# Where the softmax of the self-attention is divided by its sums: in the probabilities, head by head, instead of in the output

## The chip, the cores and the metric

The kernel runs on one core of a Trainium2 chip. The metric is the device time of one execution in microseconds. The engines are named as in the profile: PE is TensorE (matmul; PEld are its weight loads), DVE is VectorE, ACT is ScalarE, POOL is GpSimd, SP is SyncE, which issues most transfers.

## The reference

One decoder layer over x, 8 batches of 256 rows of 1024 columns: self-attention, cross-attention, feed-forward, each on a layer norm of x and added to x. Only the self-attention is touched by the change:

```python
y = einsum('bsi,oi->bso', x, sign(w / s)) * (s * scale)      # q, k, v and the output projection
scores = einsum('bhqd,bhkd->bhqk', q, k) / sqrt(32)          # 32 heads of 32, 8 key/value heads
attn = softmax(scores, axis=-1)
out = einsum('bhqk,bhkd->bhqd', attn, v)                     # then the output projection
```

The softmax divides each row of exponentials by its sum. As the division is by row (by query), it may be done to the exponentials before the product with v or to the product after it.

## The kernel before

The self-attention is done in 64 steps, one for each batch b (8) and each group c of four heads (8). A `Self` object stands for one step. The function `step(cur, prev, parts)` issues all work of one step in a fixed order; nothing is reordered afterwards, and each engine takes its instructions in the order in which they are issued. Three groups are in flight at once: `cur` gets its scores and exponentials, `prev` (one step older) gets its transposes and its product with v, and `due` (two steps older) gets its output written.

In order, a step issues the following.

- `cur.scores()` (L554): eight matmuls into four PSUM banks `s`, one for each head.
- `due.early()` (L585, L590): two matmuls with the constant `sel` spread the reciprocal sums `rT` (8 rows) over the 128 output rows, into the second half of the bank `po`; ScalarE copies them to `rb`.
- For each head, VectorE's negated row maximum `nm` (L678), and `turned(prev.p[j])` (L535, L539): four transposes of the exponentials on TensorE into one of three PSUM banks, which are also those of the projections, and a copy `pT` by ScalarE.
- `due.late()` (L600, L355, L356): VectorE multiplies the output in `po` by `rb`; ScalarE rounds the product to `oh` and VectorE takes the remainder `ol`. The output projection runs over both, `oh` and `ol`.
- The parts of the step, taken from a queue by `run_part()`: pieces of projections, layer norms and (in batch 0) weight preparation that fill TensorE while ScalarE makes exponentials. Each part carries an estimate of its length `us`. The eight exponentials of the step (`exp`, L697: two halves of rows for four heads, with the row sums collected into `sm`) are placed between the parts by these estimates: a counter `sc` starts at 1.0, grows by 0.49 for each exponential, and is compared with the sum of the parts' estimates. `run_part` also issues pieces of waiting statistics (`idle`, layer norm moments on VectorE), one for each 1.7 of estimated time. After the first part comes `prev.sums()` (L566, L568): a transpose of the eight columns of `sm` on TensorE and a copy `rT` on VectorE.
- `nc.vector.reciprocal(cur.sm, cur.sm)` (L723), and `prev.weighted(pTs)` (L574): the product with v, into the first half of `po`. The pool `pso` holds one buffer only, so `po` of the next group can be written only once that of the last is no longer read.

The usual batch has two long steps (c = 0 and 4, four or more parts of 2.0), two with layer-norm parts (c = 1 and 2) and four short ones (c = 3, 5, 6, 7, two parts of 2.0). `nan_to_num` (L362 to L368) follows each projection with work on VectorE and Pool. Cross-attention (`Cross`) runs through the same `step`, and divides its output in `late` (L659); the feed-forward follows.

Of the kernel before, what the change touches and what calls it, by code (L numbers as in the profile page):

```python
# [10 lines left out]
F32 = mybir.dt.float32  # L11
F32R = mybir.dt.float32r
U8 = mybir.dt.uint8
AF = mybir.ActivationFunctionType
ALU = mybir.AluOpType
# [3 lines left out]
P = 128  # L19
# [16 lines left out]
def decoder_layer(  # L36
# [24 lines left out]
    nc = tc.nc  # L61
    B, S, E = x.shape
    NT = B * S // P
    TB = S // P
# [15 lines left out]
    const = ctx.enter_context(tc.tile_pool(name="const", bufs=1, side="left"))  # L80
# [7 lines left out]
    pso = ctx.enter_context(tc.tile_pool(name="pso", bufs=1, space=PSUM))  # L88
    xin = ctx.enter_context(tc.tile_pool(name="x_in", bufs=4, side="left"))
    wk_ = ctx.enter_context(tc.tile_pool(name="work", bufs=1, side="left"))  # L90

    ident = const.tile([P, P], F32, name="ident")
# [3 lines left out]
    mhalf = const.tile([P, TB], F32, name="mhalf")  # L96
    nc.gpsimd.memset(mhalf, -0.5)

    sel = const.tile([8, TB, P], F32, name="sel")
    nc.gpsimd.memset(sel, 1.0)  # L100
    for t in range(TB):
        nc.gpsimd.affine_select(
            sel[:, t, :], sel[:, t, :], [[1, P]], ALU.is_ge, 0.0,
            base=4 * t * 32, channel_multiplier=-32,
        )
        nc.gpsimd.affine_select(
            sel[:, t, :], sel[:, t, :], [[-1, P]], ALU.is_ge, 0.0,
            base=31 - 4 * t * 32, channel_multiplier=32,
        )


    x1 = dram.tile([NT, P, E], F32, name="x1")
    x2 = dram.tile([NT, P, E], F32, name="x2")

# [23 lines left out]
    idle, credit = [], [0.0]  # L138
# [46 lines left out]
    def settle():  # L185
        now = list(ripe)
        ripe[:] = later
        later.clear()
        for f in now:
            f()  # L190
# [11 lines left out]

    queue = []

    def run_part():

        settle()
        p = queue.pop(0)
        p.ahead()
        if queue:  # L210
            queue[0].ahead()
        p.main()
        credit[0] += p.us
        while idle and credit[0] > 1.7:
            credit[0] -= 1.7
            idle.pop(0)()
        if not idle:
            credit[0] = 0.0
# [135 lines left out]
    def split(hi, lo, src):  # L354
        nc.scalar.copy(hi, src)  # L355
        nc.vector.tensor_sub(lo, src, hi)  # L356
# [174 lines left out]
    def turned(p):  # L531
        ps = bank([P, TB, S], "ps_pt")
        for k in range(TB):
            for t in range(TB):
                nc.tensor.transpose(  # L535
                    ps[:, k, t * P : (t + 1) * P], p[:, t, k * P : (k + 1) * P], ident
                )
        pT = wk_.tile([P, TB, S], F32, tag="pT", name="pT", bufs=4)
        nc.scalar.copy(pT, ps)  # L539
        return pT  # L540

    class Self:


        def __init__(self, st, c):
            self.st, self.c = st, c

        def scores(self):
            st, c = self.st, self.c
            s = [pss.tile([P, TB, S], F32, tag="pss", name="s") for _ in range(4)]  # L550
            for t in range(TB):
                for j in range(4):
                    p0 = 32 * j
                    nc.tensor.matmul(  # L554
                        s[j][:, t, :],
                        st.qT[p0 : p0 + 32, c, t * P : (t + 1) * P],
                        st.kT[p0 : p0 + 32, c // 4, :],
                        start=True,
                        stop=True,
                    )  # L560
            return s

        def sums(self):

            self.po = pso.tile([P, 2, S], F32, tag="pso", name="po")
            nc.tensor.transpose(self.po[:8, 1, :P], self.sm.rearrange("p t j -> p (t j)"), ident)  # L566
            self.rT = wk_.tile([8, P], F32, tag="rT", name="rT")
            nc.vector.tensor_copy(self.rT, self.po[:8, 1, :P])  # L568

        def weighted(self, pTs):  # L570
            for k in range(TB):
                for j in range(4):
                    g, p0 = 4 * (self.c // 4) + j, 32 * j
                    nc.tensor.matmul(  # L574
                        self.po[p0 : p0 + 32, 0, :],
                        self.st.v[:, k, g * HD : (g + 1) * HD],
                        pTs[j][:, k, :],
                        start=(k == 0),
                        stop=(k == TB - 1),
                    )  # L580

        def early(self):

            for t in range(TB):
                nc.tensor.matmul(  # L585
                    self.po[:, 1, t * P : (t + 1) * P], sel[:, t, :], self.rT,
                    start=True, stop=True,
                )
            self.rb = wk_.tile([P, S], F32, tag="rb", name="rb")
            nc.scalar.copy(self.rb, self.po[:, 1, :])  # L590

        def late(self):
            st, c = self.st, self.c
            if c == 0:
                i = st.b % 2
                st.oh, st.ol = [
                    [wk_.tile([P, 4, S], F32R, tag=f"{n}{i}{h}", name=n) for h in "ab"]
                    for n in ("oh", "ol")
                ]
            nc.vector.tensor_mul(self.rb, self.po[:, 0, :], self.rb)  # L600
            split(st.oh[c // 4][:, c % 4, :], st.ol[c // 4][:, c % 4, :], self.rb)

    class Cross:

# [17 lines left out]
                        )  # L622
            return s

        def sums(self):
            pass

        def weighted(self, pTs):
# [39 lines left out]
    def step(cur, prev, parts, extra=None):  # L668

        s = cur.scores()  # L670
        nm = small.tile([P, 4, TB], F32, tag="nm", name="nm")
        cur.sm = small.tile([P, TB, 4], F32, tag="sm", name="sm")
        due = prev.prev if prev is not None else None
        if due is not None:
            due.early()
        pTs = []
        for j in range(4):
            nc.vector.tensor_reduce(nm[:, j, :], s[j], AX.X, ALU.max, negate=True)  # L678
            if prev is not None:
                pTs.append(turned(prev.p[j]))  # L680
        for p in queue[: min(parts, 2)]:
            p.ahead()
        soon = [p for p in queue[:parts] if p.soon][:2]
        if isinstance(due, Cross):
            for p in soon:
                p.ahead()
        if due is not None:
            due.late()
        for p in soon:
            p.ahead()  # L690
        cur.p, cur.prev = [], prev
        exps = []

        def exp(j, t):
            if t == 0:
                cur.p.append(wk_.tile([P, TB, S], F32, tag="p", name="p", bufs=4))
            nc.scalar.activation(  # L697
                cur.p[j][:, t, :], s[j][:, t, :], AF.Exp,
                bias=nm[:, j, t : t + 1], accum_out=cur.sm[:, t, j : j + 1],
            )  # L700

        exps = [(j, t) for j in range(4) for t in range(TB)]


        pe, sc = 0.0, 1.0
        for k in range(parts):
            pe += queue[0].us
            while exps and sc < pe:
                exp(*exps.pop(0))
                sc += 0.49  # L710
            run_part()
            if k == 0 and prev is not None:
                prev.sums()
            if k == 0 and extra is not None:
                extra()
        for e in exps:
            exp(*e)
        if not parts:
            if prev is not None:
                prev.sums()  # L720
            if extra is not None:
                extra()
        nc.vector.reciprocal(cur.sm, cur.sm)  # L723
        if prev is not None:
            prev.weighted(pTs)
            prev.prev = None
        return cur
# [369 lines left out]
    for b in range(B):  # L1097
        for l in (sts, xts):
            st = State()
# [118 lines left out]
    with tc.manual_schedule(  # L1218
# [8 lines left out]
        st = sts[0]  # L1227
# [9 lines left out]
        for q in range(2 * TB):  # L1237
            t, h = q // 2, q % 2
# [30 lines left out]
        prev = None  # L1269
        for kind, sts_, plan, loads, extra, n in (  # L1270
            (Self, sts, self_plan, self_loads, self_extra, EC),
            (Cross, xts, cross_plan, cross_loads, cross_extra, XH // 4),
        ):
            for b in range(B):
                ps_ = plan(b)
                for p in ps_:
                    queue.extend(p)
                for c in range(n):
                    loads(b, c)
                    prev = step(kind(sts_[b], c), prev, len(ps_[c]), extra(b, c))  # L1280


        pairs = [(fb, f) for fb in fbs for f in range(NF)]
# [76 lines left out]
```

## Time and profile before

| | |
|---|---|
| Median of three runs | 1594.41 us (1591.75 to 1595.04) |
| The profiled execution | 1593.47 us |
| Its span in the trace | 1591.8 us |
| Mean granted TensorE clock | 0.994 |
| Self-attention, from its first scores to the first of the cross-attention | 26.3 to 674.3 us |
| Batch 0 | 101.2 us |
| Batches 1 to 7 | 77.1 to 78.9 us each |
| Mean length of steps c = 0 to 7, batches 1 to 6 | 12.3, 9.2, 9.8, 8.6, 12.6, 8.4, 8.4, 8.6 us |

A step's length is the distance between the first weight loads of the scores (L554) of two steps. In the profile a line of the timeline gives start, length, engine, source line, operation, output and inputs, and in brackets the idle time ahead of it with what ended it. A line of the waits gives who waited for whom, the total in microseconds, how many times and the longest. A line of the windows gives the stretch and its length, then for PE, PEld, DVE, ACT and POOL the busy time with the number of instructions, then the granted clock and the transfers. A matmul of 32-bit floats shows as two records for each instruction, and a transpose as one.

### The profile page before, as it was taken

The numbers are of one execution on the slowest core, as the hardware profiler recorded it, in microseconds if no ns is written. First come the engines' busy times: TensorE is split into PE (matmuls) and PEld (weight loads), VectorE is DVE, ScalarE is ACT, GpSimd is POOL, SyncE is SP. The second block draws the span as 40 slices with busy tenths as digits, with TensorE's granted clock in tenths as the row PEclk, the third lists the DMA queues.
The fourth block names the chain that finished last, engine by engine and source line by source line (L and its number), as shares of the span: only waits on it lengthen the run. The fifth ranks groups of instructions, "written<-read, shape, count | busy, mean of one in ns | idle before, by whom it ended". The sixth has DMA issues, their size and how long they took to land.

```text
span 1591.8 us, 25596 instructions
## 1 busy us (share of the span) xinstructions
PE 1550.8 (97%) x9814; PEld 1058.8 (67%) x9814; DVE 905.9 (57%) x1692; ACT 756.7 (48%) x2346; POOL 358.7 (23%) x449
## 2 busy tenths in 40 slices
PE   6899999999999999999999999999999999999998
PEld 6778888888888888777777777544444444444443
DVE  6867787868686877665676666343233323423322
ACT  4777777777777777655655666411111110111110
POOL 2333433333333343112221112100010002001102
PEclk9999999999999999999999999999999999999999
DMA  8420010101010042111154412120002002000001
GB/s 231 88 54 27 15 67 25 57 28 54 28 54 28 28 127 82 54 55 69 56 206 153 135 55 107 40 86 1 0 27 79 0 1 89 17 0 14 40 0 53
DMA packets 65610, 92.78 MB, mean 58 GB/s; under 512 B 40218, under 2 KB 46160, under 8 KB 65360
## 3 DMA queue, kind: packets, MB, share of 16 engines
q1 hardware_dynamic: 60880, 74.37, 14.9%
q0 software_dynamic: 4608, 16.78, 2.6%
q8 instruction: 77, 1.26, 0.3%
q14 instruction: 45, 0.37, 0.1%
HBM read 65.44 MB, written 25.17 MB: 57 GB/s over the span
## 4 chain that ended last, share of the span: by engine, by line
PE 62%; DVE 2%; ACT 0%; issue 0%; POOLq 0%; POOL 0%; DVEq 0%; ACTq 0%
PE ps_h L1019 19%; PE ps_z L1063 9%; PE ps_pt L535 5%; PE s L616 4%; PE po L634 4%; PE ps_p L993 3%; PE ps_o L1082 3%; PE ps_o L503 2%; PE ps_o L651 2%; PE ps_qk L848 2%; PE ps_q L833 2%; PE ps_q L410 1%; PE ps_k L784 1%; PE s L554 1%; PE ps_t L176 1%; PE po L574 1%
## 5 line engine op out<-in xcount | busy, mean ns | idle before, releaser
L697 ACT ACTIVATE p<-s,nm 128x256 f32<-128x256 f32 x768 | 356.9, 503 | 2.2 <-DVE nm L678 2.2
L539 ACT COPY pT<-ps_pt 128x512 f32<-128x512 f32 x384 | 198.2, 600 | 134.1 <-PE ps_pt L535 131.0
L1031 ACT ACTIVATE sg<-ps_h,b_col 128x512 f32<-128x512 f32 (+1 forms) x88 | 59.6, 677 | 413.5 <-PE ps_h L1019 413.5
L678 DVE TENSOR_REDUCE nm<-s 128x2 f32<-128x512 f32 x384 | 236.2, 676 | 12.6 <-PE s L616 6.7
L1032 DVE SCALAR_TENSOR_TENSOR sg<-ps_h,b_col,sg 128x512 f32<-128x512 f32 (+1 forms) x88 | 65.0, 739 | 274.9 <-ACT sg L1031 274.9
L535 PE MATMUL ps_pt<-ident,p 128*128 128x128 f32 x1536 | 195.6, 280 | 1.0 <-DVE xl L356 0.9
L535 PEld LDWEIGHTS ps_pt<-ident,p 128*128 128x128 f32 x1536 | 165.9, 142 | 26.2 <-issue 7.2
L697 ACT ACTIVATION_READ_ACCUMULATOR p<-s,nm 128x1 f32 x768 | 181.0, 236 | 0.0
L1063 PE MATMUL ps_z<-ac,u_sb 128*128 128x512 f32 x336 | 157.7, 593 | 0.0
L1092 POOL TENSOR_TENSOR x2t<-x2t,y 128x512 f32<-128x512 f32 x32 | 40.5, 1267 | 482.5 <-DVE y L1090 482.5
L410 PE MATMUL ps_q<-xh,qT_w 128*128 128x256 f32 x496 | 124.1, 291 | 0.9 <-ACT qT_w L320 0.9
L410 PE MATMUL ps_q<-xl,qT_w 128*128 128x256 f32 x496 | 119.8, 281 | 0.0
L363 POOL TENSOR_SCALAR tmp<-y 128x512 f32<-128x512 f32 x78 | 59.6, 764 | 263.8 <-DVE y L512 154.8
L1063 PEld LDWEIGHTS ps_z<-ac,u_sb 128*128 128x128 f32 x336 | 61.9, 190 | 68.8 <-issue 68.8
L503 PE MATMUL ps_o<-oT_w,oh 128*128 128x512 f32 x256 | 106.9, 417 | 0.0
L503 PE MATMUL ps_o<-oT_w,ol 128*128 128x512 f32 x256 | 101.0, 394 | 0.0
L666 POOL TENSOR_TENSOR x1t<-x1t,y 128x256 f32<-128x256 f32 x64 | 47.5, 762 | 222.9 <-DVE y L659 222.9
L410 PEld LDWEIGHTS ps_q<-xh,qT_w 128*128 128x128 f32 x496 | 93.3, 188 | 3.1 <-ACT qT_w L320 1.1
L410 PEld LDWEIGHTS ps_q<-xl,qT_w 128*128 128x128 f32 x496 | 93.5, 189 | 0.0
L554 PE MATMUL s<-kT,qT 32*128 32x256 f32 x1024 | 88.7, 413 | 2.0 <-ACT p L697 1.0
L1019 PE MATMUL ps_h<-late,w_ffn 128*128 128x512 f32 (+1 forms) x184 | 88.7, 577 | 0.0
L1019 PE MATMUL ps_h<-pT,w_ffn 128*128 128x512 f32 (+1 forms) x184 | 88.7, 577 | 0.0
(165 smaller groups left out, 2706.6 us busy)
## 6 DMA issues: line engine op xcount, KB each, us to landing
xs<-in_x_dram SPq DMA_DIRECT2D x32, 512.0 KB, 3.5
x<-xs POOLq DMA_DIRECT2D x16, 512.0 KB, 3.0
x1t<-x SPq DMA_DIRECT2D x16, 512.0 KB, 5.7
c<-in_ctx_dram SPq DMA_DIRECT2D x16, 512.0 KB, 4.0
x<-x1t POOLq DMA_DIRECT2D x16, 512.0 KB, 3.8
x2t<-x SPq DMA_DIRECT2D x16, 512.0 KB, 5.8
out_dram<-x2t SPq DMA_DIRECT2D x16, 512.0 KB, 2.6
w<-in_L_attn_q_weight_dram SPq DMA_DIRECT2D x32, 128.0 KB, 6.0
```

Source lines behind the costliest of these rows:

```text
L410: nc.tensor.matmul(ps[:, i, :], w(i, e), x_[:, e, :], start=(e == 0 and x_ is st.xh), stop=(e == EC - 1 and x_ is st.xl),)
L503: nc.tensor.matmul(ps, o_[c // 4][:, c % 4, t * P : (t + 1) * P], oT_w[:, c, h * 512 : (h + 1) * 512], start=(c == 0 and o_ is st.oh), sto ...
L535: nc.tensor.transpose(ps[:, k, t * P : (t + 1) * P], p[:, t, k * P : (k + 1) * P], ident)
L539: nc.scalar.copy(pT, ps)
L554: nc.tensor.matmul(s[j][:, t, :], st.qT[p0 : p0 + 32, c, t * P : (t + 1) * P], st.kT[p0 : p0 + 32, c // 4, :], start=True, stop=True,)
L616: nc.tensor.matmul(s[2 * i + j][:, t, :], st.cqk[p0 : p0 + XD, 2 * c + i, t * P : (t + 1) * P], st.ckv[p0 : p0 + XD, :], start=True, stop= ...
L634: nc.tensor.matmul(self.po[XD * j : XD * (j + 1), i, :], self.st.ckvT[:, k, :], pTs[2 * i + j][:, k, :], start=(k == 0), stop=(k == TB - 1),)
L678: nc.vector.tensor_reduce(nm[:, j, :], s[j], AX.X, ALU.max, negate=True)
L697: nc.scalar.activation(cur.p[j][:, t, :], s[j][:, t, :], AF.Exp, bias=nm[:, j, t : t + 1], accum_out=cur.sm[:, t, j : j + 1],)
L1019: nc.tensor.matmul(ps[h * n : h * n + n], v1_of(r, i, f, n), fb.pT[:, r, h * w_ : (h + 1) * w_], start=(r == 0), stop=(r == RC - 1),)
L1032: nc.vector.scalar_tensor_tensor(sg[:m], hs[0][:m], bg, sg[:m], ALU.add, ALU.mult)
L1063: nc.tensor.matmul(fb.zs[r], fw.u2[f // 4][:n, f % 4, r * P : (r + 1) * P], ac[:n], start=(k == 0), stop=(k == NF - 1 and COPIES < 2),)
```

## The change

The exponentials are divided in place, ahead of their transposes, and the transposed sums with all that belongs to them (`sel`, `sums`, `rT`, `rb`) are gone. In each step the reciprocal of the sums is taken for two heads at a time (`over_sums`), and each head is then multiplied by its column of `sm`, on one of three engines by the letter in `by`: P on Pool with one instruction, D on VectorE with two, A on ScalarE with two. The A heads come after all the step's exponentials and parts (`over_sums_end`). The others are issued inside `run_part`, from the second part on, as soon as the exponentials of the pair have been issued, and otherwise after the parts. The output is no longer multiplied: `early` copies it from PSUM to `oh`, and `late` subtracts that from PSUM to give `ol`. The counter `sc` starts at 0.5 in the self-attention, and the statistics are issued for each 1.4 of estimated time, also outside it.

```diff
-    sel = const.tile([8, TB, P], F32, name="sel")
-    nc.gpsimd.memset(sel, 1.0)
...
-    def run_part():
+    def run_part(then=None):
         settle()
+        if then is not None:
+            then()
...
-        while idle and credit[0] > 1.7:
-            credit[0] -= 1.7
+        while idle and credit[0] > 1.4:
+            credit[0] -= 1.4
...
+            self.by = (
+                "AAPP" if st.b == 0 else "DPAA" if c in (1, 2) else "DDAA" if c % 4 == 0 else "DDDA"
+            )
...
-        def sums(self):
-            self.po = pso.tile([P, 2, S], F32, tag="pso", name="po")
-            nc.tensor.transpose(self.po[:8, 1, :P], self.sm.rearrange("p t j -> p (t j)"), ident)
-            self.rT = wk_.tile([8, P], F32, tag="rT", name="rT")
-            nc.vector.tensor_copy(self.rT, self.po[:8, 1, :P])
+        def over_sums(self, pair):
+            heads = range(2 * pair, 2 * pair + 2)
+            r = self.sm[:, :, heads[0] : heads[-1] + 1]
+            nc.vector.reciprocal(r, r)
+            for j in heads:
+                if self.by[j] == "P":
+                    nc.gpsimd.tensor_mul(
+                        self.p[j], self.p[j],
+                        self.sm[:, :, j].unsqueeze(2).to_broadcast([P, TB, S]),
+                    )
+                elif self.by[j] == "D":
+                    for t in range(TB):
+                        p = self.p[j][:, t, :]
+                        nc.vector.tensor_scalar_mul(p, p, self.sm[:, t, j : j + 1])
+
+        def over_sums_end(self):
+            for j in range(4):
+                if self.by[j] == "A":
+                    for t in range(TB):
+                        p = self.p[j][:, t, :]
+                        nc.scalar.activation(p, p, AF.Copy, scale=self.sm[:, t, j : j + 1])
         def weighted(self, pTs):
+            self.po = pso.tile([P, S], F32, tag="pso", name="po")
...
         def early(self):
-            for t in range(TB):
-                nc.tensor.matmul(
-                    self.po[:, 1, t * P : (t + 1) * P], sel[:, t, :], self.rT,
-                    start=True, stop=True,
-                )
-            self.rb = wk_.tile([P, S], F32, tag="rb", name="rb")
-            nc.scalar.copy(self.rb, self.po[:, 1, :])
...
+            nc.scalar.copy(st.oh[c // 4][:, c % 4, :], self.po)
         def late(self):
...
-            nc.vector.tensor_mul(self.rb, self.po[:, 0, :], self.rb)
-            split(st.oh[c // 4][:, c % 4, :], st.ol[c // 4][:, c % 4, :], self.rb)
+            nc.vector.tensor_sub(
+                st.ol[c // 4][:, c % 4, :], self.po, st.oh[c // 4][:, c % 4, :]
+            )
...
-        pe, sc = 0.0, 1.0
+        divided = isinstance(cur, Self)
+        pe, sc = 0.0, 0.5 if divided else 1.0
+        pairs = [0, 1]
         for k in range(parts):
...
-            run_part()
-            if k == 0 and prev is not None:
-                prev.sums()
+            def then():
+                while k and divided and pairs and len(exps) <= 4 - 4 * pairs[0]:
+                    cur.over_sums(pairs.pop(0))
+            run_part(then)
...
         for e in exps:
             exp(*e)
...
-        nc.vector.reciprocal(cur.sm, cur.sm)
+        for i in pairs:
+            cur.over_sums(i)
+        cur.over_sums_end()
```

For the cross-attention `over_sums` takes the one reciprocal where it was before, and `over_sums_end` does nothing.

More of the change, by code (lines that the diff above doesn't have):

```diff
@@ L97, in decoder_layer @@
     nc.gpsimd.memset(mhalf, -0.5)
-    sel = const.tile([8, TB, P], F32, name="sel")
-    nc.gpsimd.memset(sel, 1.0)
-    for t in range(TB):
-        nc.gpsimd.affine_select(
-            sel[:, t, :], sel[:, t, :], [[1, P]], ALU.is_ge, 0.0,
-            base=4 * t * 32, channel_multiplier=-32,
-        )
[L106 to L109, printed above, removed]
     x1 = dram.tile([NT, P, E], F32, name="x1")
@@ L574, in weighted @@
                     nc.tensor.matmul(
-                        self.po[p0 : p0 + 32, 0, :],
+                        self.po[p0 : p0 + 32, :],
                         self.st.v[:, k, g * HD : (g + 1) * HD],
@@ L582, in early @@
         def early(self):
-            for t in range(TB):
-                nc.tensor.matmul(
-                    self.po[:, 1, t * P : (t + 1) * P], sel[:, t, :], self.rT,
-                    start=True, stop=True,
-                )
-            self.rb = wk_.tile([P, S], F32, tag="rb", name="rb")
-            nc.scalar.copy(self.rb, self.po[:, 1, :])
-        def late(self):
             st, c = self.st, self.c
@@ L599, in late @@
                 ]
-            nc.vector.tensor_mul(self.rb, self.po[:, 0, :], self.rb)
-            split(st.oh[c // 4][:, c % 4, :], st.ol[c // 4][:, c % 4, :], self.rb)
+            nc.scalar.copy(st.oh[c // 4][:, c % 4, :], self.po)
+        def late(self):
+            st, c = self.st, self.c
+            nc.vector.tensor_sub(
+                st.ol[c // 4][:, c % 4, :], self.po, st.oh[c // 4][:, c % 4, :]
+            )
     class Cross:
@@ L623, in scores, with over_sums, over_sums_end @@
             return s
-        def sums(self):
+        def over_sums(self, pair):
+            if pair:
+                nc.vector.reciprocal(self.sm, self.sm)
+        def over_sums_end(self):
             pass
@@ L717, in step @@
             exp(*e)
[L718 to L722, printed above, removed]
-        nc.vector.reciprocal(cur.sm, cur.sm)
+        for i in pairs:
+            cur.over_sums(i)
+        cur.over_sums_end()
+        if not parts and extra is not None:
+            extra()
         if prev is not None:
```

## The prediction

> **What bounds the kernel now.** I read the page's busy table first, then a table of busy time for one batch of the self-attention, then the timeline of one of its steps engine by engine, then the waits of TensorE.
>
> ```profile
> PE 1550.8 (97%) x9814; PEld 1058.8 (67%) x9814; DVE 905.9 (57%) x1692; ACT 756.7 (48%) x2346; POOL 358.7 (23%) x449
> 282.70:360.90 78.20, 77.54 (x701) 64.34 (x697) 59.68 (x121) 57.38 (x192) 29.45 (x30) 1.00 0.12 42
> ```
>
> The second line is batch 3 (eight steps, from its first scores to the next batch's): TensorE (first pair) is busy 77.5 of 78.2 us, VectorE (third) 59.7, ScalarE (fourth) 57.4, Pool 29.5. Batches 2 to 6 read alike within 0.2 us. TensorE sets the pace, but the two others have only 20 us a batch to spare, 2.5 us a step. One step, batch 3's seventh, on TensorE:
>
> ```profile
> 342.90 1.07 PE L574 MATMUL po<-pT,v 128*32 128x256 f32 x16
> 343.90 1.20 PE L554 MATMUL s<-kT,qT 32*128 32x256 f32 x16
> 344.87 0.60 PE L585 MATMUL po<-rT,sel 8*128 8x128 f32 x4
> 345.40 1.99 PE L535 MATMUL ps_pt<-ident,p 128*128 128x128 f32 x16
> 347.22 0.38 PE L410 MATMUL ps_q<-xh,qT_w 128*128 128x256 f32 x1
> ...
> 349.10 0.28 PE L410 MATMUL ps_q<-xl,qT_w 128*128 128x256 f32 x1
> 349.21 0.27 PE L566 MATMUL po<-ident,sm 128*8 128x128 f32 x1
> 349.24 0.36 PE L410 MATMUL ps_q<-xh,qT_w 128*128 128x256 f32 x1
> 349.44 0.27 PE L410 MATMUL ps_q<-xl,qT_w 128*128 128x256 f32 x1
> ...
> 352.31 1.07 PE L554 MATMUL s<-kT,qT 32*128 32x256 f32 x10
> ```
>
> Columns are start, length, operation. There is no gap: weighted sums, scores, the broadcast of the sums (L585), the transposes of four heads, 32 projection matmuls, 8.41 us from scores to scores. Matmuls overlap, so a cost is the distance from one start to the next, not a length. ScalarE in the same step:
>
> ```profile
> 343.68 0.24 ACT L697 ACTIVATION_READ_ACCUMULATOR p<-s,nm 128x1 f32 x1
> 345.55 0.37 ACT L590 COPY rb<-po 128x256 f32<-128x256 f32 x1 [1.64 <-issue]
> 346.10 2.06 ACT L539 COPY pT<-ps_pt 128x512 f32<-128x512 f32 x4 [0.17 <-PE ps_pt L535]
> 348.01 0.44 ACT L355 CAST oh<-rb 128x256 fp32r<-128x256 f32 x1
> ```
>
> After its last exponential ScalarE stands 1.64 us, until TensorE has done L585. That hole recurs in most steps (idle before L590: 99.0 us in 48 steps by L590's own record). VectorE has its hole too: its subtraction L356 waits for oh in all 64 steps, 37.9 us together. And what TensorE waits for:
>
> ```profile
> PEld s L554 <- ACT p L697: 14.3, 38, 0.6
> PEld po L566 <- DVE rb L600: 5.4, 7, 1.4
> PEld po L574 <- DVE rT L568: 1.9, 1, 1.9
> ```
>
> **The change part by part.** The sum is made against the profiled execution, 1593.47 us (span 1591.76 and 1.7 around it); the median of the runs is 0.94 above that.
>
> *Removed from TensorE.* L585 (two instructions a step, four passes): 344.87 to 345.40, 0.53 us, the same in other steps. L566: the pair 349.10 to 349.24 holds one normal spacing of 0.11, and the next spacing is 0.20 for 0.12, so it costs 0.03 + 0.08 = 0.11 us. Together 0.64 x 64 steps = 41.0 us. Part of the L585 distance may be the turn from short to full rows, which stays: four plain spacings of 0.113 give 0.45, then 36 us. I take 38.
>
> *Waits removed.* L566 waited for L600, because both use the one bank of po, 5.4 us; the weighted sums once waited for rT, 1.9 us. Both vanish: 7. In short steps (four microseconds of projections) the eighth exponential now stands ahead of the two y copies of the projection on ScalarE instead of behind them, since the count starts at 0.5 for 1.0; the scores no longer wait for it: of the 14.3 us of weight-load waits about 5 are real (the scores' start in 352.31 against the end of the weighted sums), the rest is hidden by the pipeline. Gains so far 38 + 7 + 5 = 50.
>
> *Added to ScalarE.* "A" heads, two activations each: 2 x 2 in batch 0's steps, two heads in steps 0, 1, 2, 4 of the others and one in steps 3, 5, 6, 7, 24 instructions a batch. Nearest row: y<-ps_q (L419, a copy scaled by a column, 128x256), 504 ns long, in pairs 0.36 apart. So 0.36 x 24 = 8.6 us a batch; removed is rb (8 x 0.37 = 3.0). ScalarE goes from 57.4 to 63 of about 73. In the step above they fit the hole: weighted sums 1.0, scores 1.0, the first head's transposes 0.45 and the hand-over 0.17 make 2.6 us from the end of the parts to the first pT copy; ahead of it ScalarE has two y (0.17 + 0.80), one A head 0.72, oh 0.37: 2.1. With two A heads and no y after the exponentials 2.1 likewise; with two and y, 2.8, in the first step of a batch only, where it costs 0.2. oh is copied from PSUM as soon as the weighted sums are there, ahead of the transposes' copies, where formerly it lay after them: nothing behind it waits longer.
>
> *Added to VectorE.* "D" heads: two multiplications each, 36 a batch. The nearest row is kT<-kT (L447, 128x256, 293 ns); xn (L168, two columns as operands) stands 0.455 apart where z<-y (L362, constants, same size) stands 0.343, so a column costs about 0.11; 0.21 + 0.11 = 0.32 us each, 11.5 us. One more reciprocal a step, 8 x 0.11. Removed: rT 8 x 0.2, rb 8 x 0.35. Net 8 us, 60 to 68 of 73. But the subtraction no longer stands waiting for oh (37.9/64 = 0.6 a step, 4.7 a batch) nor rT for L566 (16.3 us in all), so the time to get through VectorE's queue grows by 1 to 2 us a batch only. New are two waits in the queue: each reciprocal waits for the exponentials of its pair, and behind it stand the output multiplication of the projection (it frees a PSUM bank), z, fin and the next step's maxima. In a short step the second reciprocal can run about when the parts end, and delays those by the one D head, 0.6 us; the maxima are then done 1 us later, still before the last pT copy, which the exponentials follow anyway. The steps with layer normalization (1 and 2) are VectorE's fullest, 8.7 of 9.2; they receive one D head only, and the count of 1.4 for 1.7 moves two statistics instructions (0.65 each) out of step 1 into the two before it.
>
> *Added to Pool.* "P" heads, a product of 128x512: nearest row the sums L364, 1.32 us; two a step in batch 0 and one in steps 1 and 2. Heads 2 and 3 are transposed 3.2 us after the parts end at the earliest, and their exponentials end before the last part: 2.6 + 0.3 is covered. Pool is busy 29 of 78. The five instructions for sel at the start go: they lie beside the loads, nothing. SP's queue is unchanged.
>
> *A rule that speaks against it.* Six times v<-y took 0.83 us on VectorE where z<-y of the same shape takes 0.426:
>
> ```profile
> 178.89 0.83 DVE L362 TENSOR_SCALAR v<-y 128x512 f32<-128x512 f32 x1
> 178.16 1.27 POOL L517 TENSOR_TENSOR xs<-xs,z 128x512 f32<-128x512 f32 x1 [0.85 <-DVE z L368]
> ```
>
> Pool's addition had started and ended at 179.43; v ended 0.29 later. The Trainium skill, "SBUF — State Buffer", "Who interferes with whom", says why: both share a port pair, and a VectorE instruction in a two-port mode waits for the whole of a Pool instruction that came first. The D products are of this kind. By the plain rows the sum has 0 for this; by the rule each group of D products can be held up by the rest of a Pool instruction: Pool is busy 3.3 of 8.4 us in a short step, so 0.4 x 0.6 = 0.25 us a group, some 3 us of VectorE a batch. It has 5 to spare. I take 2 us on the path for all batches.
>
> *New waits in all.* Batch 0, where ScalarE ends each step with weight copies and four A products for the heads that are transposed first: 0.5 a step, 4. Steps 1 and 2 of six batches, 0.3 each, 4. The first step of seven batches 0.2, and the port 2: 3.5. Total 11.5; bounds 0 and 40.
>
> Sum: 1593.5 - 50 + 11.5 = 1555; beside the median 1556, rounded towards less gain, **1557 us**.
>
> **The rivals.**
> *Half of it eaten.* ScalarE becomes the bound in short steps: 8 exponentials 3.6, four pT copies 1.9, y 0.8, A 0.72, oh 0.37 = 7.4 us for a TensorE step of 7.75. If an A product costs 0.5 (its length, not its spacing) and the reciprocal's answer comes 0.3 late, that is 8.0, and only 0.4 of 8.41 is gained; the fuller steps 1 and 2 gain nothing. 28 short steps x 0.4 + 28 others x 0.2 = 17: 1577. For it: ScalarE's queue is in order. Against: the 1.64 us hole.
> *Slower, by the port pair.* If each group of D products meets a fresh Pool instruction (1.3 us, two groups a short step), VectorE's short step is 6.0 + 1.5 + 2.6 = 10.1 us, and TensorE waits for the maxima and the divided heads: +1.7 in 28 short steps, 48, while the other 36 save 0.6 each, 22, and 10 of other waits vanish: about 1610. It decides once the mean block exceeds some 1.6 us a short step. Against: z<-y shows 426 ns in all 32, and in the step above Pool runs from 343.86 to 346.03 and from 350.54 to 351.83, of which only the second touches the time of the products.
> *The change does not do what it says:* the transposes start late because the division now lies between exponentials and transposes, yet TensorE had nothing to do there anyway, so no change. It would need over 2.6 us of division after the last exponential in nearly all steps; 1594.
>
> **How the numbers follow.** Main case 0.70 (1545 to 1568); still better, all waits gone, 0.04 (1540); half eaten 0.14 (1568 to 1588); no change 0.03; slower 0.09. The range 1542 to 1583 holds the main case and most of the second. Faster by over 0.2% (3.2 us, about what a measurement of this kernel can tell from no change) 0.88, same 0.03, slower 0.09.
>
> **What would show it.** Right: a short step of 7.7 to 7.9 us on TensorE with scores followed by transposes at once; a batch of 73 to 74.5; A products 0.36 apart in the former hole; VectorE busy near 68 a batch and no wait before its subtraction. Wrong: TensorE's weight loads of the transposes waiting for p from VectorE, ScalarE or Pool by more than 12 us in total; D products of 0.7 us or more beside Pool; steps 1 and 2 longer than 9.2. Cross-attention and feed-forward (from 674 us on) should be as long as before.

## The result and the profile after: 21 us gained of the 37 forecast

| | before | after |
|---|---|---|
| Median of four runs | 1593.08 us | 1571.75 us (1571.54 to 1573.56) |
| Ratio | | 0.9868 (95% interval 0.9851 to 0.9885) |
| Span of the profiled execution | 1591.8 us | 1569.9 us |
| Batch 0 | 101.2 us | 108.3 us |
| Batch 1 | 77.1 us | 73.3 us |
| Batches 2 to 6, each | 78.2 us | 74.5 us |
| Batch 7 | 78.8 us | 74.2 us |
| Cross-attention, first to last scores | 334.7 us | 333.0 us |

The gain is 21.3 us by the medians. It lies inside the range of the prediction (1542 to 1583), but 15 us above its number, 1557, and outside the 1545 to 1568 that the main case gave itself. By size it fell among the values of the rival "half of it eaten"; whether by its mechanism is settled below. Steps are numbered by c from here on: step 6 is the seventh of a batch.

The page after, with the line of busy time, and the row of batch 3 in the table of stretches (stretch, length, then PE, PEld, DVE, ACT and POOL busy, granted clock, transfers):

```profile
PE 1513.1 (96%) x9494; PEld 1015.9 (65%) x9494; DVE 973.0 (62%) x1880; ACT 811.4 (52%) x2482; POOL 390.5 (25%) x474
281.68:356.20 74.52, 72.68 (x660) 59.26 (x656) 68.74 (x150) 63.96 (x207) 31.85 (x32) 1.00 0.12 44
```

TensorE lost 37.7 us of work over the span, of which only 21.9 came off the span: TensorE waits more than before. VectorE stands at 68.7 a batch and ScalarE at 64.0, where the prediction had 68 and 63. Batch 3's step 6 on TensorE, to be laid beside the one shown for before:

```profile
340.43 1.15 PE L547 MATMUL s<-kT,qT 32*128 32x256 f32 x16
341.50 1.99 PE L524 MATMUL ps_pt<-ident,p 128*128 128x128 f32 x16
343.32 0.39 PE L399 MATMUL ps_q<-xh,qT_w 128*128 128x256 f32 x1
...
347.10 0.28 PE L399 MATMUL ps_q<-xl,qT_w 128*128 128x256 f32 x1
347.31 1.07 PE L584 MATMUL po<-pT,v 128*32 128x256 f32 x16
348.31 0.50 PE L547 MATMUL s<-kT,qT 32*128 32x256 f32 x4
```

The transposes follow the scores at once. The step lasts 348.31 - 340.43 = 7.88 us; it lasted 8.41. Here the change does what it says. What the other engines do just then:

```profile
340.11 0.18 DVE L560 RECIPROCAL sm<-sm 128x4 f32<-128x4 f32 x1 [0.40 <-ACT p L708]
340.33 0.91 ACT L577 ACTIVATE p<-p,sm 128x256 f32<-128x256 f32 x2 [0.25 <-DVE sm L560]
340.40 0.62 DVE L570 TENSOR_SCALAR p<-p,sm 128x256 f32<-128x256 f32 x2
341.14 0.35 ACT L601 CAST oh<-po 128x256 fp32r<-128x256 f32 x1
342.19 2.05 ACT L528 COPY pT<-ps_pt 128x512 f32<-128x512 f32 x4 [0.70 <-PE ps_pt L524]
```

The A products and `oh` stand in ScalarE's former hole, and 0.70 us of it is left. The three D heads are divided by 341.02, before their transposes.

TensorE's waits up to the cross-attention's start, by contrast, hold three entries that were nothing, 1.1 and 0.3 us before (total, times, longest):

```profile
PE ps_pt L524 <- ACT pT L528: 6.6, 8, 1.1
PE ps_d L334 <- POOL dg L327: 6.4, 2, 4.0
PE ps_t L163 <- DVE xn L155: 4.4, 6, 0.8
```

They belong to three places: batch 0, the step after a long one (c = 1, 9.23 to 9.66 us in batches 2 to 6), and the step after the layer norms (c = 3, 8.64 to 9.03). A fourth is batch 7. The experiments take them one by one.

### The profile page after: what moved, and what is told of

Same layout as the page of the kernel before. It is cut to its first block, busy times and chain, and to the rows that moved or that the text cites. A ratio compares the mean times of both kernels' runs of the same rounds, so it can differ in the third digit from the quotient of the medians.

```text
span 1569.9 us, 25667 instructions
## 1 busy us (share of the span) xinstructions
PE 1513.1 (96%) x9494; PEld 1015.9 (65%) x9494; DVE 973.0 (62%) x1880; ACT 811.4 (52%) x2482; POOL 390.5 (25%) x474
## 4 chain that ended last, share of the span: by engine, by line
PE 77%; DVE 14%; ACT 6%; DMA 1%; issue 1%; POOL 0%; SPq 0%; POOLq 0%; DVEq 0%; ACTq 0%
PE ps_h L1034 19%; PE ps_z L1078 9%; PE ps_pt L524 8%; PE ps_o L492 5%; PE ps_q L399 5%; PE s L622 4%; PE po L645 4%; PE ps_p L1008 4%; DVE nm L689 4%; PE ps_o L1097 3%; ACT p L708 3%; PE s L547 2%; PE po L584 2%; PE ps_o L662 2%; PE ps_qk L863 2%; DVE p L570 2%
## 5 line engine op out<-in xcount | busy, mean ns | idle before, releaser
L524 PEld LDWEIGHTS ps_pt<-ident,p 128*128 128x128 f32 x1536 | 164.4, 141 | 51.8 <-issue 21.9
L708 ACT ACTIVATION_READ_ACCUMULATOR p<-s,nm 128x1 f32 x768 | 189.8, 247 | 0.0
L1107 POOL TENSOR_TENSOR x2t<-x2t,y 128x512 f32<-128x512 f32 x32 | 40.5, 1267 | 482.5 <-DVE y L1105 482.5
L570 DVE TENSOR_SCALAR p<-p,sm 128x256 f32<-128x256 f32 x252 | 99.0, 448 | 9.6 <-DVE sm L560 1.4
L577 ACT ACTIVATE p<-p,sm 128x256 f32<-128x256 f32 x200 | 87.8, 512 | 17.8 <-DVE sm L560 17.6
```

Source lines behind the costliest of these rows:

```text
L524: nc.tensor.transpose(ps[:, k, t * P : (t + 1) * P], p[:, t, k * P : (k + 1) * P], ident)
L570: nc.vector.tensor_scalar_mul(p, p, self.sm[:, t, j : j + 1])
L577: nc.scalar.activation(p, p, AF.Copy, scale=self.sm[:, t, j : j + 1])
L708: nc.scalar.activation(cur.p[j][:, t, :], s[j][:, t, :], AF.Exp, bias=nm[:, j, t : t + 1], accum_out=cur.sm[:, t, j : j + 1],)
```

## The experiments

### Batch 0: what stands behind Pool's products

Pool's timeline in batch 0's first step, and the matmuls that stand next on TensorE:

```profile
33.75 2.04 POOL L563 TENSOR_TENSOR p<-p,sm 128x512 f32<-128x512 f32 x2 [0.21 <-DVE sm L560]
35.77 1.22 POOL L327 TENSOR_SCALAR dg<-ident,scol 128x128 f32<-128x128 f32 x2
33.65 0.41 PE L466 MATMUL ps_v<-vT_w,xl 128*128 128x256 f32 x1
36.45 1.39 PE L334 MATMUL ps_d<-dg,ones 128*128 128x128 f32 x4 [2.39 <-POOL dg L327]
```

`dg` is a diagonal of weight scales that the look-ahead of a part (`ahead`) lays on Pool. `run_part` issues the division of a pair (`then`) before that look-ahead. So `dg`, which was ready to be made, stands in Pool's queue behind two products that wait for exponentials. In c = 6 the same wait lasts 4.0 us.

A second loss sits on it. The granted clock in the same stretches, after:

```profile
32.00:42.40 10.40, 7.33 (x33) 6.53 (x33) 2.07 (x6) 2.58 (x9) 4.45 (x10) 0.51 0.82 162
117.40:124.40 7.00, 4.77 (x24) 3.94 (x28) 3.35 (x5) 1.06 (x2) 5.83 (x8) 0.51 0.00 0
```

The clock (third number from the end) is half for about 10 and 7 us, and the L466 matmuls stand 0.21 us apart instead of 0.12. Before had 0.85 and 1.00 in these two rows. The experiment moves one call:

```diff
     def run_part(then=None):
         settle()
-        if then is not None:
-            then()
         p = queue.pop(0)
...
             queue[0].ahead()
+        if then is not None:
+            then()
         p.main()
```

> The changed kernel with the in-place division of a pair issued after the look-ahead work of the parts instead of before it, so that in batch 0 the diagonal tiles dg stand ahead of the P products in Pool's queue. Theory (Pool's queue: TensorE waits for dg behind products that wait for exponentials, 6.4 us in two steps, and its clock is then granted at half for 6.8 us more twice): the first and seventh step of batch 0 come from 18.6 and 17.3 to about 14 and 13, batch 0 from 108.3 to 97, the time from 1571.7 to about 1561. Rival (batch 0 loses because the A products for the heads that are transposed first end too late): batch 0 stays at 105 or more, time 1569 or more. Batches 1 to 7 alike in both.

Measured: 1565.69 us (ratio 0.9831, 0.9817 to 0.9846), batch 0 101.7 us (steps 0 and 6: 18.61 and 17.29 became 14.29 and 13.44, before had 13.84 and 13.43), the other batches as after. The same two stretches and the wait that is left, of this kernel:

```profile
32.00:42.40 10.40, 9.59 (x70) 8.57 (x71) 5.40 (x11) 5.52 (x16) 6.41 (x14) 0.84 0.84 173
117.40:124.40 7.00, 6.59 (x62) 5.28 (x54) 4.84 (x9) 6.17 (x20) 4.58 (x9) 1.00 0.01 2
```

```profile
PE ps_d L334 <- POOL dg L327: 1.9, 3, 1.1
```

The order on Pool's queue is the cause of 6.6 of the 7.1 us that batch 0 had lost, 6.1 us of the median, and most of the half clock in these two stretches went with the waits; the rival, A products that end too late, wanted 105 us or more for the batch. It is not all that was expected (97 us): step 7 grew from 8.78 to 10.38, and why was not looked into.

### How much there was to gain, and what the division costs

```diff
-            for j in heads:
+            for j in ():
...
-            for j in range(4):
+            for j in ():
```

> The changed kernel with the products by the reciprocal sums left out on all three engines (the reciprocals are still taken), so the output is not divided: what the removal from TensorE and the removed waits are worth with none of the added work but the reciprocals. If the prediction's gains of 50 us were sized right: 1543 to 1546. If the removal was over-sized (36 for the two groups of matmuls and little for the waits): 1553 to 1557.

Measured: 1553.03 us (0.9752, 0.9733 to 0.9770). Batch 0 is 99.7 us, batches 2 to 6 73.6, batch 7 69.4. So without any product 40 us are gained, not 50; and the division costs 1571.75 - 1553.03 = 18.7 us. By the batches' lengths it is 8.6 in batch 0, about 5 in batches 1 to 6 together, and 4.8 in batch 7.

This kernel also tells which of the late steps the division causes: c = 3 falls from 9.03 to 7.94, but c = 1 is 9.59 without one product. So the products do not make c = 1 late.

### The two counts, without the rest

The first of these puts both new counts into the kernel before, the second only the exponentials' 0.5.

```diff
-        while idle and credit[0] > 1.7:
-            credit[0] -= 1.7
+        while idle and credit[0] > 1.4:
+            credit[0] -= 1.4
...
-        pe, sc = 0.0, 1.0
+        pe, sc = 0.0, 0.5 if isinstance(cur, Self) else 1.0
```

> The kernel before with the two counts of the change alone: exponentials placed from 0.5 instead of 1.0 in the self-attention, statistics for each 1.4 instead of 1.7. The division stays in the output. If the counts bring part of the gain by themselves (scores no longer wait for the last exponential, as the prediction had it): the short steps lose up to 0.2 us and the time is 1588 to 1591. If the statistics' new place costs as in the changed kernel: the second step grows by some 0.5 and the time is 1593 to 1596.

Measured: 1601.16 us (1.0069, 1.0050 to 1.0089). Its waits:

```profile
PEld po L566 <- DVE rb L600: 17.5, 21, 2.4
PE po L566 <- DVE rb L600: 11.2, 6, 2.0
```

The page of before had 5.4 in the first of these rows. The sums' transpose writes the bank that `rb` is read from, so TensorE was tied to VectorE's place in its queue; more work ahead of `rb` on VectorE makes TensorE wait.

> The kernel before with the one count of the exponentials, 0.5 for 1.0 in the self-attention. The prediction put 5 us on the scores that no longer wait for the last exponential. If that was right by itself: 1586 to 1588. If only the fourth and eighth steps of a batch change, as in the run with both counts (0.2 and 0.15): 1589 to 1591. If it costs in other steps: 1593 or more.

Measured: 1596.10 us in 12 runs (1.0020, 1.0009 to 1.0031), no gain and if anything a small loss. The 5 us that the prediction gave to the earlier exponentials are not there by themselves. In the profile of this run the short steps 5 and 6 last 8.35 and 8.41 us in batches 2 to 6, as before, only step 7 is shorter by 0.15, and the wait that was to vanish is as long as before:

```profile
PEld s L554 <- ACT p L697: 14.3, 38, 0.4
```

How the loss of the two counts divides between them wasn't tried further: the 1.4 alone was not run in the kernel before.

### Step 1: statistics ahead of the maxima

The profile after, batch 3's step 1, which starts at 293.37:

```profile
295.55 0.64 DVE L138 BATCH_NORM_STATS2 st<-xs 128x6 f32<-128x512 f32 x1
296.11 2.46 DVE L689 TENSOR_REDUCE nm<-s 128x2 f32<-128x512 f32 x4
298.49 0.54 DVE L155 TENSOR_SCALAR xn<-xs,mv,rs 128x512 f32<-128x512 f32 x1
299.17 0.63 PE L163 MATMUL ps_t<-ident,xn 128*128 128x128 f32 x4 [0.78 <-DVE xn L155]
```

The maxima begin 2.74 us into the step (before: about 1.4), and TensorE's layer-norm transposes wait 0.78 for `xn` behind them. Two theories: the count of 1.4 put the statistics there, or VectorE has no time left over these steps, wherever they stand. The first run goes back to 1.7, the second on to 1.0.

```diff
-        while idle and credit[0] > 1.4:
-            credit[0] -= 1.4
+        while idle and credit[0] > 1.7:
+            credit[0] -= 1.7
```

> The changed kernel with one statistics instruction for each 1.7 of estimated part time, as before, instead of 1.4. Theory (statistics moved to the end of a batch's first step stand ahead of the maxima on VectorE and make the second step late): the second step of batches 2 to 6 comes from 9.65 to about 8.9, 4 us in all, time about 1567.5. Rival (the second step is over-full on VectorE by the division itself): it stays at 9.6 or grows, since a statistics instruction comes back into it; time 1571 or more.

Measured: 1575.96 us (0.9895, 0.9880 to 0.9909). Step 1 of batches 2 to 6 came to 8.71, as expected, but step 2 went from 8.93 to 10.68; the maxima began 1.26 into step 1, and now TensorE waits in step 2:

```profile
PE ps_pt L524 <- DVE xl L345: 8.5, 5, 1.8
```

> The changed kernel with one statistics instruction for each 1.0 of estimated part time instead of 1.4, so that those of a batch end early in its first step instead of in its last part. Theory (it is their place ahead of the maxima at the end of the first step that makes the second step late): the second step of batches 2 to 6 comes from 9.66 to about 8.75 and the third does not grow (at 1.7 it grew to 10.68), 4.5 us, time about 1567. Rival (VectorE is short of time over the first three steps, wherever the statistics stand): what one step gains another loses, time 1571 to 1573.

Measured: 1571.20 us (0.9873, 0.9858 to 0.9888); step 1 is 9.52 us, not 8.75. By its number this is the second theory. But the edit did not clear the place. From the `qT` that VectorE begins 8 to 9 us into step 0 up to the maxima of step 1, its queue in batches 2 to 6 holds five statistics instructions in the profile after and five with 1.0; with 1.7 it holds three, as in the kernel before. And the run without products has five too, so it tells the two theories apart. Its steps 0 and 1 of batch 3 start at 271.81 and 283.64:

```profile
280.10 0.43 DVE L351 TENSOR_SCALAR qT<-y 128x512 f32<-128x512 f32 x1 [0.55 <-ACT y L408]
281.20 1.27 DVE L138 BATCH_NORM_STATS2 st<-xs 128x6 f32<-128x512 f32 x2
282.63 0.64 DVE L138 BATCH_NORM_STATS2 st<-xs 128x6 f32<-128x512 f32 x1
284.89 0.68 DVE L138 BATCH_NORM_STATS2 st<-xs 128x6 f32<-128x512 f32 x1
285.73 0.64 DVE L138 BATCH_NORM_STATS2 st<-xs 128x6 f32<-128x512 f32 x1
286.28 2.46 DVE L689 TENSOR_REDUCE nm<-s 128x2 f32<-128x512 f32 x4
```

VectorE stands idle for 0.55 us just ahead of this `qT`, and then works without a gap to the maxima, which begin 2.64 us into step 1. Over the two steps it has 2.3 us to spare. The profile after, the same two steps:

```profile
281.68:293.37 11.69, 11.69 (x117) 10.51 (x113) 11.05 (x26) 8.71 (x29) 5.10 (x6) 1.00 0.01 2
293.37:303.02 9.65, 8.87 (x76) 6.59 (x72) 9.47 (x22) 8.91 (x28) 4.58 (x6) 1.00 0.37 129
```

Here VectorE (third) is busy 20.5 of 21.3 us and has 0.8 to spare, and step 1 is late by nearly the same amount. So neither the products nor the spare time decide it. The first theory stands: what makes step 1 late is the work that stands in VectorE's queue between the last projections and the maxima, and the count of 1.4 put two more statistics there. The run with 1.0 did not test it. Where the statistics could stand without costing elsewhere stays open: with 1.7, step 2 paid for it.

### Step 3: the port pair

The profile after, from step 2 into step 3 (which starts at 311.96):

```profile
309.49 1.29 POOL L506 TENSOR_TENSOR xs<-xs,z 128x512 f32<-128x512 f32 x1 [3.83 <-DVE sm L560]
310.74 1.09 POOL L563 TENSOR_TENSOR p<-p,sm 128x512 f32<-128x512 f32 x1
309.57 2.41 DVE L570 TENSOR_SCALAR p<-p,sm 128x256 f32<-128x256 f32 x2
311.90 0.68 DVE L345 TENSOR_TENSOR xl<-ps_t,xh 128x512 fp32r<-128x512 f32 x1
312.50 0.16 DVE L560 RECIPROCAL sm<-sm 128x4 f32<-128x4 f32 x1
312.70 1.71 ACT L577 ACTIVATE p<-p,sm 128x256 f32<-128x256 f32 x4 [1.04 <-DVE sm L560]
315.20 1.06 PE L524 MATMUL ps_pt<-ident,p 128*128 128x128 f32 x8 [0.81 <-ACT pT L528]
```

The pair of D products starts 0.08 us after Pool's addition and lasts 2.41 us, where an undisturbed pair lasts 0.62 (shown above, at 340.40). Its two products take 1.36 and 1.13 us, and each ends 0.15 after one of Pool's two instructions. Behind it the remainder `xl`, the second reciprocal, ScalarE's A products and step 3's transposes are late in turn. The rival was that ScalarE's A products make the step late by themselves. The edit gives both heads to Pool, whose second product would then be the one to be late.

```diff
-                "AAPP" if st.b == 0 else "DPAA" if c in (1, 2) else "DDAA" if c % 4 == 0 else "DDDA"
+                "AAPP" if st.b == 0 else "PPAA" if c in (1, 2) else "DDAA" if c % 4 == 0 else "DDDA"
```

> The changed kernel with PPAA for DPAA in the second and third step of batches 1 to 7: Pool instead of VectorE divides the first head. Theory (the D product of the third step is held up by two Pool instructions in turn, 2.41 us for a pair of 0.62, and the fourth step starts late): the fourth step of batches 1 to 6 comes from 9.03 to about 8.1, 5.5 us in all, time about 1566. Rival (the fourth step is late because of ScalarE's A products): it stays at 9.0, time 1571.

Measured: 1568.48 us (0.9848, 0.9833 to 0.9863), step 3 9.03 to 8.39 (8.10 was expected), step 1 unchanged at 9.66. The same place in this kernel:

```profile
309.83 1.29 POOL L506 TENSOR_TENSOR xs<-xs,z 128x512 f32<-128x512 f32 x1 [3.15 <-DVE sm L560]
310.13 0.69 DVE L345 TENSOR_TENSOR xl<-ps_t,xh 128x512 fp32r<-128x512 f32 x1 [0.33 <-ACT xh L344]
311.08 2.05 POOL L563 TENSOR_TENSOR p<-p,sm 128x512 f32<-128x512 f32 x2
311.51 0.18 DVE L560 RECIPROCAL sm<-sm 128x4 f32<-128x4 f32 x1 [0.69 <-ACT p L708]
311.89 1.71 ACT L577 ACTIVATE p<-p,sm 128x256 f32<-128x256 f32 x4
```

Counted from the start of step 2 (303.30 here, 303.02 in the profile after), `xl` runs at 6.8 us instead of 8.9, beside Pool's addition, and the A products begin at 8.6 instead of 9.7. The block of one pair of D products is a cause, worth 3.3 us of the median; the A products are the same in both runs. The step is 7.94 without products, so 0.45 us stay with the other products.

### Batch 7: the shares follow c, the parts do not

In batch 7 other parts run in the same steps, and without products c = 4, 5 and 7 fall from 10.16, 10.31 and 9.88 to 8.77, 8.83 and 7.61. Other shares for this batch:

```diff
-                "AAPP" if st.b == 0 else "DPAA" if c in (1, 2) else "DDAA" if c % 4 == 0 else "DDDA"
+                "AAPP" if st.b == 0
+                else ("PPAA" if c in (3, 4) else "DPPA" if c > 4 else "DDAA" if c == 0 else "DDDA")
+                if st.b == 7
+                else "DPAA" if c in (1, 2) else "DDAA" if c % 4 == 0 else "DDDA"
```

> The changed kernel with other shares in batch 7 alone: PPAA in its fourth and fifth step (its layer-norm steps) and DPPA in the sixth to eighth, where Pool has nothing to do. Without any division these five steps took 42 us in all, with it 47. Theory (the shares of the other batches put the D products into the steps where VectorE is fullest): about 3 to 4 us come back, time 1568. Rival (ScalarE's A products and pT copies are the limit there): 1571 to 1572.

Measured: 1573.68 us (0.9888, 0.9871 to 0.9904), batch 7 74.6 us. Steps 4 and 5 gained 1.4 and 1.0 us; step 3 lost 1.0 and step 7 lost 1.8. The expectation failed: in part the wait moved to the heads that were given to Pool, for which TensorE's weight loads now wait 2.5 us in this batch and did not wait before. That the division costs 4.8 us in this batch stands by the run without products; which part of it stands behind which instruction stays open.

### All together, and one step further

The late division issue, `"AADD"` for Pool's heads in batch 0's steps 0 and 6, Pool for D in steps 1 and 2, batch 7's shares and the count 1.0:

```diff
+                ("AADD" if c in (0, 6) else "AAPP") if st.b == 0
+                else ("PPAA" if c in (3, 4) else "DPPA" if c > 4 else "DDAA" if c == 0 else "DDDA")
+                if st.b == 7
+                else "PPAA" if c in (1, 2) else "DDAA" if c % 4 == 0 else "DDDA"
```

> The causes mended together: pairs divided after the look-ahead work; AADD for AAPP in the first and seventh step of batch 0; PPAA in the second and third step of batches 1 to 6; the shares of the run with other shares in batch 7; statistics for each 1.0. If the causes add: 1571.7 less 8 (batch 0), 3.5 (two fuller steps), 4 (statistics), 3.5 (batch 7), about 1553, which is what the kernel without any division took. If they share a limit on VectorE or ScalarE: 1558 to 1562.

Measured: **1554.96 us** (0.9773, 0.9758 to 0.9788), 16.8 us less than the change as made and the fastest of all but the one that leaves the products out. Batch 0 takes 100.8, batches 2 to 6 73.0, batch 7 73.1 us. It stands 1.9 us above the kernel without products: nearly all of the division's cost can be put where it hides. The sum of the expectation came out near, its terms did not all: step 1 stayed late, batch 7 gained 1.1 us of 3.5, and step 3 gained 1.1 us where D taken out of steps 1 and 2 alone had brought 0.6. Steps 0 to 3 of batches 2 to 6 are 11.69, 9.54, 8.70 and 7.91.

Step 1 is still late. The next edit takes D out of step 0 too, on the theory that VectorE lacks time over steps 0 and 1:

```diff
-                else "PPAA" if c in (1, 2) else "DDAA" if c % 4 == 0 else "DDDA"
+                else "PPAA" if c in (0, 1, 2) else "DDAA" if c % 4 == 0 else "DDDA"
```

> The kernel with the causes mended together, and PPAA for DDAA in the first step of batches 1 to 6 too, so that VectorE has four products (1.3 us) less there. Theory (VectorE is busy without a gap from a batch's first step into its second, and what is taken from it there comes off the second step): the second step of batches 2 to 6 comes from 9.54 to about 8.8, 3.7 us, time about 1551. Rival (the statistics have to stand behind the last projection's work anyway, and VectorE would only wait earlier): 9.5, time 1555.

Measured: 1559.15 us (0.9789, 0.9774 to 0.9804). This interval overlaps the last one, but the steps tell it: step 1 of batches 2 to 6 grew from 9.54 to 10.30. Two views of this kernel, its timeline and TensorE's waits (its longer expression for the shares puts the lines that follow it three further down):

```profile
280.15 2.05 POOL L566 TENSOR_TENSOR p<-p,sm 128x512 f32<-128x512 f32 x2 [4.42 <-DVE sm L563]
281.23 1.25 DVE L351 TENSOR_SCALAR qT<-y 128x512 f32<-128x512 f32 x1 [0.55 <-ACT y L408]
```

```profile
PE ps_t L163 <- DVE xn L155: 7.0, 6, 1.4
```

Pool's two products are running when VectorE comes to `qT`, which takes 1.25 us for 0.41 elsewhere. This is the `qT` with which the work ahead of the maxima begins, so the maxima and step 1 are later by nearly as much. Giving Pool the products took work from VectorE where it had time and gave it a wait where it had none.

## Why the prediction was right in its direction and 15 us off in its number

Its sum, against the span: 50 gained, 11.5 lost, 38.5 net. The runs: 40 gained without products, 18.7 lost to them, 21.3 net. Both terms were mis-sized, and each for its own reason. That the range held the result it owes to the values of a rival whose mechanism did not come about, and so to luck.

- **The removal, 38 forecast.** Mechanism right. A clean step went from 8.34 to 7.82 or from 8.41 to 7.88, so 0.52 to 0.53 a step, 33.5 us over 64 steps. That is the spacing of L585 alone. The further 0.11 for L566 cannot be seen in these steps, and both ends of the prediction (36 and 41) were too high.
- **The waits, 7, and the exponentials' count, 5.** The waits of L566 for `rb` and of L574 for `rT` are gone. The 5 is the step that failed: it took a part of the weight-load waits for path, and the count for their cause. With the count alone they stay at 14.3 us and nothing is gained (1.0020), and 11.1 us of them are left in the profile after. With 33.5 and 7 the sum is 40.5, beside the 40 of the run without products. That agreement is in part luck: 1.6 of the 40 lie in the cross-attention, and the clean steps of that run are 7.87 to 7.98.
- **A products, 0.36 apart in the hole.** Measured: four in 1.70 us, some 0.40 apart, in the hole. ScalarE's 64.0 a batch stands beside 63. So the rival "half of it eaten" did not come about: it wanted 8.0 us in a short step, and the short step is 7.8 to 7.9. The time fell near its 1577 by other causes.
- **D products, 0.32 each.** Undisturbed they stand 0.26 us apart (in the profile after, the pair at 281.59 is followed by `qT` at 282.12), so the term was a little high. But 35 of the 252 last from 0.6 to 1.37 us instead of 0.35. That VectorE's 68.7 a batch meets the forecast 68 is thus in part luck.
- **The subtraction no longer waits for `oh`.** So it was; the 37.9 us of idle time before it are gone.
- **The port rule.** The Trainium skill, "SBUF — State Buffer", "Who interferes with whom", was weighed as a mean: 0.25 us a group, some 3 us of VectorE a batch, 2 us on the path for all batches. The trace bears its rule out (1.36 and 1.13 us for products of 0.35, each ending behind a Pool instruction), and the mean too: what the D products last beyond 0.35 us adds up to 2.9 to 4.5 us a batch. The path is what was mis-sized. The blocks fall on the same steps in each of batches 1 to 6. In steps 3, 6 and 7 one product is held nearly every time (0.85, 0.92 to 1.34 and 0.70 us), and it costs steps 6 and 7 nothing that can be seen: they last 7.88 and 7.89. In step 2 the output projection's addition to x and Pool's product meet both products of the pair. Taking D out there, and in step 1, which stayed as long, was worth 3.3 us of the median. Blocks of 0.7 us or more had been named as a sign of being wrong.
- **Statistics: "moves two out of step 1 into the two before it".** Counted as a help; the reading of the queue failed. They stood ahead of step 1's maxima. Step 2 gained what step 1 lost (9.95 to 8.93, 9.23 to 9.66), so the two together still gained 0.6 of the 1.04 us that L585 had cost in them. Going back to 1.7 made it worse, though, as step 2 then took 10.68. "5 to spare" a batch says nothing of a place in the queue. The step longer than 9.2 us, named as a sign of being wrong, came with 9.66.
- **"Pool: covered".** The largest miss. The P products were asked whether they end in time, not what stands behind them in Pool's queue. `dg` does, and TensorE waited 6.4 us for it, with the clock at half. The prediction gave batch 0 a loss of 4, for a net gain of some 2 us by its terms of each step; batch 0 lost 7.1.
- **Batch 7** was treated as the others; the products cost 4.8 us there.
- **Waits of the transposes for p, over 12 us as a sign of being wrong**: they stayed below that (3.3 us in weight loads for the A heads, 1.2 us in matmuls for the D heads). The waits moved to `dg`, `xn` and `pT` instead. Feed-forward took the same time as before, 582.9 us from the last scores of the cross-attention on; the cross-attention itself gained 1.7 us, which the prediction had at nothing.

## What to carry to other kernels

When an instruction that waits is put into a queue, list what stands behind it on that engine, on Pool and in start-up stages too, and who waits for that: here one call moved past another was worth 6 us. Spare time, even over the few steps in which the new work stands, does not tell what a queue taken in order will do: step 1 was late by nearly the same amount with 2.3 us to spare in 21 as with 0.8. What counts is what stands in the queue between the arrival of an input and the instruction that others wait for. Work moved to Pool is not free for VectorE if both then use the port pair at the same moment, so a share is settled by running it in its own step.

## What the runs showed of the hardware that was not expected

- A pair of VectorE products beside two Pool instructions one behind the other was held twice, each product by one of them: 2.41 us for 0.62.
- Pool multiplied a head of 128x512 by broadcast columns in 1.04 us, less than its plain addition of two tiles of that size (1.29); the prediction took 1.32 for it.
- Two waits of TensorE of 2.4 and 4.0 us in batch 0 lie in stretches of half clock of about 10 and 7 us. The first stretch had begun before its wait, as it did in the kernel before, where it ended after some 3 us (0.85 over 10.4 us); with the waits shortened the clock was back near the values of before (0.84 and 1.00). In batch 7 the kernel before had such a stretch of 7 us too (663 to 670 us), just behind a wait of 1.7 us for `rT`, and the kernel after has none there. The run with the exponentials' count alone has this wait but no such stretch, and its last step of the batch takes 8.09 us instead of 11.25. So up to 3 of the 4.6 us that batch 7 gained may be the clock's; no run took it apart.
